# A five-layer convolution and attention kernel: the start of the attention stage, its first image, put in another order

## The chip, the cores and the metric

The kernel runs on one core of one Trainium2 chip, in one launch. The metric is the device time in microseconds (us), the median of several runs. Names of engines are those of the profile: PE is the TensorE matmul engine, PEld its weight loads, DVE is VectorE, ACT is ScalarE, POOL is GpSimd, SP is SyncE. Lines such as L1475 are lines of the kernel before.

## The reference, cut to what matters

Sixteen images of 256 channels and 28x28 pixels go through a binary 3x3 convolution, a second block of a 3x3 and a 1x1 binary convolution with gates, a third block of two binary 3x3 convolutions with batch norms, and attention over the pixels of each image. The end of the third block and the attention are where the change lies:

```python
    out = batchnorm(out, g3, b3)      # over all images: (x - m) * rsqrt(v + EPS) * g + b
    out = out + x                     # x: the input of this third block
    return prelu(out, a3)             # where(y >= 0, y, a3 * y)
...
    q = jnp.einsum('rc,bcn->bnr', Wq, xf)        # 64 rows out of 256 channels, 784 pixels
    k = jnp.einsum('rc,bcn->brn', Wk, xf)
    v = jnp.einsum('rc,bcn->bnr', Wv, xf)
    attn = jnp.einsum('bnr,brm->bnm', q, k) * scale
    attn = jax.nn.softmax(attn, axis=-1)
    out = jnp.einsum('bnm,bmr->brn', attn, v)
    out = jnp.einsum('cr,brn->bcn', Wp, out)
    return out.reshape(B, C, H, W) + x
```

The batch norm's statistics need the last convolution of the last image. So the first image's attention can start only once they are there.

## The kernel before, in words

`forward` runs the stages one after the other. An image is held as two channel halves of 128 partitions (`k` = 0, 1) by 784 pixels; the pixels in turn come in two halves of 392 (`cuts`, below "half one" and "half two", HN = 392). The products of the last convolution land in `pt`, the tiles that the profile calls `p`; the third block's input is `x2`, for the first two images loaded back into SBUF during the stage before (L488), for the others in DRAM as `x2d`.

After the last convolution `forward` issues `keep_busy(35)`, 35 matmuls of 128x512 on an idle tile whose result nobody reads (L502), and beside them `norm("l2c", ...)` (L234): DVE aggregates the statistics, ACT takes the square root (L143, in `rsqrt`), DVE makes the scale `sg3` (the profile's `l2c_r`) from it, and ACT makes the shift `bg3` (`l2c_shift`, L260).

`attend_unshifted` does the attention. Inside its `manual_schedule` each engine keeps the order in which the program issues its instructions, so the order of the Python calls is the order on each queue. The pieces that the change and the prediction name:

- Image 0 is made by hand (L1620 to L1630). Scale and x2 in one DVE step for channel half 1 (L1622, `x*sg3 + x2`, in both pixel halves first). Then, for each pixel half: `finish_a` on ACT for channel half 0 (L1453, `x*sg3 + bg3`), ACT's shift of channel half 1 (L1626), DVE's addition of x2 to channel half 0 (L1627), DVE's prelu of both channel halves (L1629, `max(alpha*y, y)`, which reads y twice), and `queries_keys` on PE (L1475): two fp32 matmuls of 128x128x392 give queries in PSUM partitions 0 to 63 and keys in 64 to 127 of one bank.
- An ACT instruction on two columns with `AF.Exp` (L1631) brings in the exp table ahead of its first use, and `keep_busy(8)` issues 8 more idle matmuls on PE (L1468).
- `keys_to` and `queries` copy keys and queries out of PSUM: keys twice, to partitions 64 to 127 by ACT and to 0 to 63 by DVE (both L1486), queries by ACT (L1482).
- `finish_a(1)` and `finish_b(1)` do the same for image 1 with all 784 pixels: ACT's `x*sg3 + bg3` (L1453), DVE's addition (L1461) and prelu (L1462). For images from 2 on, `finish_a` ends with a DMA on POOL's queue that adds x2d to the tile (L1455).
- `scores(b, c)` is chunk c of 7: two fp32 matmuls side by side (L1498) into a tile of the pool `ps_sc`, which has two buffers, and ACT's exp of 128x784 (L1502) into one of seven `es` buffers.
- `project_v` makes the values (L1561, 16 small matmuls, 32 in the profile, since it lists an fp32 matmul as two), ACT copies them (L1565), DVE transposes them (`turn_v`, L1571). `values(b, c)` multiplies them with an `es` chunk (L1519, tile `av`).
- `sum_up` adds `es` chunks: 0 to 3 on POOL (L1510, L1512), 4 to 6 on DVE.

Then comes the loop over b from 0 to 14. Pass b does the rest of image b's chunks, and makes image b+1's queries, keys and values, and images b+2 and b+3's `finish_b` and `finish_a`, in between.

```python
            scores(b, 1)
            ...
            scores(b, 3)
            sum_up(b, 2, 3)
            ps = two_banks(psmi, "mi")
            for h in range(2):
                queries_keys(b + 1, h, ps)
```

Of the kernel before, what the change touches and what calls it, by code (L numbers as in the profile page):

```python
# [27 lines left out]
F32 = mybir.dt.float32  # L28
# [5 lines left out]
AF = mybir.ActivationFunctionType  # L34
# [5 lines left out]
P = 128  # L40
# [46 lines left out]
def forward(ctx: ExitStack, tc: tile.TileContext, d: dict, out: bass.AP, careful: bool):  # L87
# [16 lines left out]
    def pv(name):  # L104
        return vec[:, VECS.index(name), :]
# [31 lines left out]
        V.tensor_tensor(o, a, b, op)  # L137
        return o

    def rsqrt(name, v, half=None, beside=None):  # L140

        r, t = (const.tile(list(v.shape), F32, name=name + q) for q in ("_r", "_t"))
        A.activation(t, v, AF.Sqrt)  # L143
        if beside:
            beside()
        V.reciprocal(r, t)
        tt(t, r, r, ALU.mult)
        if half is not None:
            tt(r, r, half, ALU.mult)
        else:  # L150
            V.tensor_scalar(r, r, -0.5, None, ALU.mult)
        tt(t, t, v, ALU.mult)
        V.scalar_tensor_tensor(r, t, -3.0, r, ALU.add, ALU.mult)
        return r
# [76 lines left out]
                V.bn_aggr(self.mv[:, k, :], self.fin[:, k, :])  # L231
            return self.mv[:, :, 0], self.mv[:, :, 1]

    def norm(name, moments, gamma, beta, sf=None, then=lambda r: None, late=False):  # L234


        half, e = vtile(name + "_half"), vtile(name + "_e")
        V.tensor_scalar(half, gamma, -0.5, None, ALU.mult)
        if sf is not None:

            tt(e, sf, sf, ALU.mult)
            V.tensor_scalar(e, e, 1e-30, 1.0 / EPS, ALU.max, ALU.mult)
            V.reciprocal(e, e)
        m, var = moments()
        v, c, less = vtile(name + "_v"), vtile(name + "_c"), vtile(name + "_less") if late else None
        if sf is not None:
            tt(v, var, e, ALU.add)
        else:
            V.tensor_scalar(v, var, EPS, None, ALU.add)
        r = rsqrt(name, v, half, (lambda: V.tensor_scalar(less, m, -1.0, None, ALU.mult)) if late else None)  # L250
        then(r)
        if not late:
            tt(c, m, r, ALU.mult)
            return r, tt(c, beta, c, ALU.subtract)

        def shift(b):
            o = vtile(f"{name}_shift{len(made)}")
            made.append(o)
            for k in range(2):
                A.activation(o[:, k:k + 1], r[:, k:k + 1], AF.Identity, bias=b[:, k:k + 1], scale=less[:, k:k + 1])  # L260
            return o

        made = []
        return r, shift
# [225 lines left out]
    with tc.tile_pool(name="ps_conv", bufs=3, space=PSUM) as psc, \  # L490
# [7 lines left out]
        def keep_busy(n):  # L498

            ps = pss.tile([P, 512], F32, tag="sm", name="unused")  # L500
            for _ in range(n):
                tc.keep_in_program_order(T.matmul(ps, lhsT=idle[:, 0:P], rhs=idle, start=True, stop=True))  # L502
# [706 lines left out]
        with tc.tile_pool(name="ph2", bufs=1) as ph:  # L1209
# [119 lines left out]
            if careful:  # L1329
                keep_busy(45)  # L1330
                sg3, bg3 = norm("l2c", mom, pv("g3"), pv("b3"), sf2)
                tt(bg3, bg3, cc, ALU.add)
            else:
                keep_busy(35)
                with tc.manual_schedule(engines={ET.DVE, ET.Activation}):
                    sg3, shift3 = norm("l2c", mom, pv("g3"), pv("b3"), sf2, late=True)
                    bg3 = shift3(b3c)


# [69 lines left out]
def attend_unshifted(ctx, tc, d, out, wqk, wv, wp, keys, worst, doubts, flag, pv, finish):  # L1409
# [40 lines left out]
    def finish_a(b, n=slice(0, N), ks=range(2)):  # L1450
        for k in ks:
            v = x[b][:, k, n]
            A.activation(v, v, AF.Identity, bias=bg3[:, k:k + 1], scale=sg3[:, k:k + 1])  # L1453
        if b >= 2 and 1 in ks:
            nc.gpsimd.dma_start(out=x[b], in_=x2d[b], accum_op=ALU.add)  # L1455
# [8 lines left out]
    def keep_busy(n):  # L1464

        ps = one_bank(pssm, "sm")
        for _ in range(n):
            T.matmul(ps, lhsT=idle[:, 0:P], rhs=idle, start=True, stop=True)  # L1468

    qs = [None] * B  # L1470

    def queries_keys(b, h, ps):

        for k in range(2):
            T.matmul(  # L1475
                ps[:, h, :HN], lhsT=wqk[:, k, :], rhs=x[b][:, k, h * HN:(h + 1) * HN], start=(k == 0), stop=(k == 1)
            )

    def queries(b, h, ps):
        if h == 0:  # L1480
            qs[b] = buf("q", 2, shape=(P, HN))
        A.copy(qs[b][64 * h:64 * h + 64], ps[0:64, h, :HN])  # L1482

    def keys_to(b, rows, h, ps):
        copy = A.copy if rows else V.tensor_copy
        copy(  # L1486
            keys[b % 2][64 * rows:64 * rows + 64, :, 2 * h:2 * h + 2, 0:GC].rearrange("p c g i -> p g c i"),
            ps[64:P, h, :HN].rearrange("p (g c i) -> p g c i", g=2, i=GC),
        )
# [80 lines left out]
    def turn_v(b):  # L1570
        V.transpose(va[b % 2].rearrange("p c r -> p (c r)"), vt.rearrange("p c a i -> p (c a i)"))  # L1571
# [44 lines left out]
    with tc.manual_schedule(engines={ET.PE, ET.Activation, ET.DVE, ET.Pool, ET.SP}):  # L1616

        ps = [two_banks(psmi, "mi"), two_banks(pssc, "sc")]
        cuts = [slice(h * HN, h * HN + HN) for h in range(2)]
        for n in cuts:  # L1620
            v = x[0][:, 1, n]
            V.scalar_tensor_tensor(v, v, sg3[:, 1:2], x2[0][:, 1, n], ALU.mult, ALU.add)  # L1622
        for h, n in enumerate(cuts):
            finish_a(0, n, (0,))
            v, w = (x[0][:, k, n] for k in range(2))
            A.activation(w, w, AF.Identity, bias=bg3[:, 1:2])  # L1626
            V.tensor_tensor(v, v, x2[0][:, 0, n], ALU.add)  # L1627
            for k, y in enumerate((v, w)):
                V.scalar_tensor_tensor(y, y, alpha[:, k:k + 1], y, ALU.mult, ALU.max)  # L1629
            queries_keys(0, h, ps[h])  # L1630
        A.activation(ph.tile([P, 2], F32, name="e"), sg3, AF.Exp, scale=0.0)  # L1631
        keep_busy(8)
        for h in range(2):
            keys_to(0, 1, h, ps[h])
            queries(0, h, ps[h])
            keys_to(0, 0, h, ps[h])
        finish_a(1)
        scores(0, 0)
        project_v(0)
        finish_b(1, ks=(0,))  # L1640
        turn_v(0)
        finish_b(1, ks=(1,))
        V.transpose(ones.rearrange("p a i -> p (a i)"), turned.rearrange("p a i -> p (a i)"))
        for b in range(B - 1):
            scores(b, 1)
            if b > 0:
                take_values(b - 1)
            if b == 0:
                finish_a(2)
            if b > 1:  # L1650
                project(b - 2, 0)()
            sum_up(b, 1)
            scores(b, 2)
            if b > 0:
                sum_up(b - 1, 6)
            scores(b, 3)
            sum_up(b, 2, 3)
            ps = two_banks(psmi, "mi")
            for h in range(2):
                queries_keys(b + 1, h, ps)  # L1660
            for h in range(2):
                keys_to(b + 1, 1, h, ps)
            for h in range(2):
                queries(b + 1, h, ps)
            for h in range(2):
                keys_to(b + 1, 0, h, ps)
            project_v(b + 1)
            if b > 0:
                sum_all(b - 1)
            turn_v(b + 1)  # L1670
            scores(b, 4)
            scores(b, 5)
            sum_up(b, 5)
            if b + 2 < B:
                finish_b(b + 2)
            if b + 3 < B:
                finish_a(b + 3)
            for c in range(4):
                values(b, c)
            if b > 0:  # L1680
                denominators(b - 1)
                invert(b - 1)
                normalize(b - 1)
            scores(b, 6)
            scores(b + 1, 0)
            if b > 1:
                project(b - 2, 1)()
                store(b - 2)
            if b > 0:
                watch(b - 1)  # L1690
            for c in range(4, NC_):
                values(b, c)


        b = B - 1
        scores(b, 1)
        take_values(b - 1)
        project(b - 2, 0)()
        sum_up(b, 1)
        scores(b, 2)  # L1700
        denominators(b - 1)
        invert(b - 1)
        scores(b, 3)
        sum_up(b, 2, 3)
        normalize(b - 1)
        scores(b, 4)
        scores(b, 5)
        sum_up(b, 5)
        scores(b, 6)
        project(b - 2, 1)()  # L1710
        store(b - 2)
        doubts_so_far()
        for mo in range(2):
            project(b - 1, mo, pool=pssc)()
        store(b - 1)
        watch(b - 1)
        for c in range(3):
            values(b, c)
        last = two_banks(pssc, "sc")
        denominators(b)  # L1720
# [214 lines left out]
```

## Time and profile before

| what | value |
|---|---|
| median of three runs | 949.11 us (948.44 to 949.25) |
| the profiled execution's own time | 949.33 us |
| its span in the profile | 947.5 us |
| PE busy | 930.7 us (98%) |
| DVE, ACT, POOL busy | 757.1, 675.1, 139.0 us |
| mean granted TensorE clock | 0.999 |
| idle matmuls ahead of attention, L502 | 35, from 661.07 us to 668.64 us |
| first attention matmul | 668.73 us |
| end of the queries and keys of image 0 | 671.79 us |
| queries and keys of image 1 begin | 678.65 us |

Times within the run are counted from the span's start. The span is 1.8 us shorter than the profiled execution's device time, and that execution is 0.2 us above the median. In the views that follow, a line of the chain of work gives start, length, and engine with tile and line; a line of the timeline gives start, length, engine, line, operation, out<-in, shapes, count and, in brackets, the idle time ahead of it with what ended it. Lengths in the timeline count a group of instructions from the first one's start to the last one's end.

### The profile page before, as it was taken

To read this page: it belongs to the slowest core of one execution; us is meant where nothing else is said; L and a number is where in the kernel's file an instruction comes from. 1 tells how busy PE (TensorE), PEld (TensorE's weight loads), DVE (VectorE), ACT (ScalarE), POOL (GpSimd) and SP (SyncE) were. 2 spreads that over 40 slices of the span, in tenths; PEclk is the share of its full clock that TensorE was granted. 3 is DMA by queue.
4 is the path that set the end of the run, shared out by engine and by line. 5 is a ranking of instruction groups with operands and counts; after the bars stand their busy time and mean duration, and the time that the engine had idled before them with its cause. 6 is when DMAs were issued, how large, how long until landed. Compare 5 with 4: busy or idle time off the path is not lost.

```text
span 947.5 us, 15043 instructions
## 1 busy us (share of the span) xinstructions
PE 930.7 (98%) x5636; PEld 583.2 (62%) x5636; DVE 757.1 (80%) x1446; ACT 675.1 (71%) x1179; POOL 139.0 (15%) x157
## 2 busy tenths in 40 slices
PE   7999999999999999999999999999999999999996
PEld 3555678788888878887555565556444444444442
DVE  3777798999998899987788878889656768687765
ACT  5665578888888888875777766775867666666652
POOL 2001100000000000000000000000334353534331
PEclk9999999999999999999999999999999999999999
DMA  9887434445533444421556211111132434434212
GB/s 346 287 303 264 168 121 138 165 181 198 198 139 139 148 156 164 160 86 50 223 209 214 113 40 59 79 78 59 35 68 70 112 92 94 112 78 126 69 68 106
DMA packets 39333, 130.70 MB, mean 138 GB/s; under 512 B 4866, under 2 KB 16324, under 8 KB 39252
## 3 DMA queue, kind: packets, MB, share of 16 engines
q1 hardware_dynamic: 33332, 98.31, 28.7%
q0 software_dynamic: 5632, 30.54, 11.7%
q8 instruction: 46, 0.75, 0.3%
q10 hardware_dynamic: 288, 0.80, 0.2%
q14 instruction: 35, 0.29, 0.1%
HBM read 72.67 MB, written 32.11 MB: 111 GB/s over the span
## 4 chain that ended last, share of the span: by engine, by line
PE 94%; DMA 1%; ACT 1%; DVE 1%; SPq 1%; issue 0%; DVEq 0%; ACTq 0%
PE cv L400 29%; PE cv L806 29%; PE sc L1498 8%; PE av L1519 8%; PE cv L933 5%; PE mi L1475 5%; PE sm L1561 2%; PE mi L1579 2%; PE unused L502 2%; PE sm L1519 1%; DMA xs<-in_x_dram 1%; PE gate L901 1%; PE hid L709 1%; DMA shifted<-fpads 1%; SPq L293 0%
## 5 line engine op out<-in xcount | busy, mean ns | idle before, releaser
L806 PE MATMUL cv<-vs,w 128*128 128x392 f32 (+1 forms) x1296 | 272.4, 352 | 0.3 <-DVE vs L137 0.3
L400 PE MATMUL cv<-fpads,wpk 128*128 128x392 f16 (+1 forms) x1458 | 247.8, 326 | 2.5 <-DVE wpk L325 1.2
L400 PEld LDWEIGHTS <-wpk 128*128 128x128 f16 x1782 | 171.5, 97 | 123.2 <-issue 3.1
L806 PEld LDWEIGHTS cv<-vs,w 128*128 128x128 f32 x768 | 143.2, 190 | 6.3
L1502 ACT ACTIVATE es<-sc 128x784 f32<-128x784 f32 x112 | 87.3, 822 | 41.4 <-PE sc L1498 41.4
L806 PEld LDWEIGHTS <-w 128*128 128x128 f16 x768 | 69.4, 99 | 51.9 <-issue 9.1
L1498 PE MATMUL sc<-q,keyswa 64*128 64x392 f32 x448 | 89.9, 513 | 0.9 <-ACT es L1502 0.9
L1519 PE MATMUL av<-es,v 128*64 128x392 f32 x448 | 80.7, 499 | 0.0
L1264 DVE SCALAR_TENSOR_TENSOR p<-ab,vec 128x392 f32<-128x392 int16 (+1 forms) x132 | 78.0, 605 | 0.0
L416 ACT ACTIVATE ab<-cv 128x392 int16<-128x392 f32 (+1 forms) x66 | 32.1, 486 | 56.3 <-PE cv L400 53.4
L1512 POOL TENSOR_TENSOR sum<-sum,es 128x784 f32<-128x784 f32 x32 | 67.2, 2099 | 3.1 <-ACT es L1502 0.6
L1498 PEld LDWEIGHTS sc<-q,keyswa 64*128 64x128 f32 x448 | 38.9, 186 | 44.0 <-issue 17.1
L400 PE MATMUL cv<-shifted,wpk 128*128 128x392 f16 (+1 forms) x324 | 60.6, 322 | 0.2 <-DMA shifted<-fpads 0.2
L806 PE MATMUL cv<-one_on,w 128*128 128x392 bf16 x240 | 59.4, 329 | 0.0
L961 POOL DMA_DIRECT2D x2d<-x x16 | 8.6, 536 | 345.3 <-DVE x L955 285.0
L1486 DVE COPY keyswa<-mi 64x392 f32<-64x392 f32 x31 | 16.3, 564 | 53.1 <-ACT q L1482 53.1
L1519 PEld LDWEIGHTS av<-es,v 128*64 128x64 f32 x448 | 29.4, 136 | 47.4 <-issue 47.0
L418 DVE SCALAR_TENSOR_TENSOR ab<-ab,cv 128x392 int16<-128x392 int16 (+1 forms) x66 | 36.0, 546 | 27.7 <-ACT ab L416 27.3
L788 ACT CAST vs<-vs 128x840 fp32r<-128x840 bf16 x63 | 54.1, 882 | 2.5 <-DVE vs L137 2.5
L933 PE MATMUL cv<-z,fw 128*128 128x392 f32 x256 | 48.9, 342 | 0.1
L933 PEld LDWEIGHTS cv<-z,fw 128*128 128x128 f32 x256 | 46.1, 188 | 0.9 <-ACT z L925 0.9
L1475 PE MATMUL mi<-p,wqk 128*128 128x392 f32 x124 | 45.1, 506 | 0.1
(323 smaller groups left out, 1531.2 us busy)
## 6 DMA issues: line engine op xcount, KB each, us to landing
xs<-in_x_dram SPq DMA_DIRECT2D x30, 784.0 KB, 5.1
one_on<-vs SPq DMA_DIRECT2D x60, 209.8 KB, 2.8
x2d<-x POOLq DMA_DIRECT2D x16, 784.0 KB, 3.6
out_dram<-p SPq DMA_DIRECT2D x15, 784.0 KB, 3.4
shifted<-fpads SPq DMA_DIRECT2D x26, 449.8 KB, 2.8
p<-x2d POOLq DMA_DIRECT2D x14, 784.0 KB, 6.7
p<-x2d SPq DMA_DIRECT2D x13, 784.0 KB, 5.7
n0d<-n POOLq DMA_DIRECT2D x16, 392.0 KB, 4.8
```

The source lines that it names most:

```text
L400: T.matmul(pss[j][:, n // size if careful else h, :rows * S].rearrange("p (a b) -> p a b", b=S), lhsT=w[:, n, c, :], rhs=src[:, blocks[j][ ...
L416: A.activation(by_halves(ab[:, 1], blocks[j]), ps, AF.Copy, scale=1.0 / PACK)
L418: V.scalar_tensor_tensor(a, b, -PACK, ps, ALU.mult, ALU.add)
L788: copy(v, w)
L806: T.matmul(ps.rearrange("p (a b) -> p a b", b=S), lhsT=w[:, k, c, u, mo * P:(mo + 1) * P], rhs=one_on[:, u, k, :, 0:S] if moved and c == 1 ...
L933: T.matmul(ps[:, h, :HN], lhsT=w[:, k, mo * P:(mo + 1) * P], rhs=z2[b][:, k, h * HN:(h + 1) * HN], start=(k + i == 0), stop=(k + i == 2),)
L1264: V.scalar_tensor_tensor(p, y, alpha[:, mo:mo + 1], y, ALU.mult, ALU.max, accum_out=mom.sums_at(at, mo)[0] if mom.by_sums(at, mo) else None,)
L1475: T.matmul(ps[:, h, :HN], lhsT=wqk[:, k, :], rhs=x[b][:, k, h * HN:(h + 1) * HN], start=(k == 0), stop=(k == 1))
L1498: T.matmul(ps[:, h, :HN], lhsT=chunk[rows], rhs=qs[b][rows], start=True, stop=True)
L1502: A.activation(e, ps[:, :, :HN], AF.Exp, scale=0.125)
L1512: (V if late else nc.gpsimd).tensor_tensor(sums[b, late], sums[b, late], e, ALU.add)
L1519: T.matmul(ps[64 * h:64 * h + 64, :HN], lhsT=w, rhs=e[:, h, :], start=start, stop=stop)
```

## The change

It is confined to the first image of attention and what leads to it. The norm's `rsqrt` gets an extra ACT instruction of two columns with `AF.Exp` right behind the square root, and the one at L1631 goes. The idle matmuls go from 35 to 31, and the 8 at L1468 go. Channel half 0 of pixel half one is made in the way of channel half 1 (one DVE step with scale and x2, then ACT's shift), as is channel half 1 of image 1. Pixel half two of image 0 gets its queries and keys by separate 64-column matmuls in two PSUM tiles (`queries_keys_apart`), of which the one for keys comes from `ps_sc`. The keys of half one are copied by ACT alone, those of half two by DVE alone. Image 0's values (`project_v`, `turn_v`) come ahead of its scores, chunks 0 to 3 of its scores and the first two of `values` come ahead of the loop, and `finish_a(2)` with its DMA on POOL's queue comes after `sum_up(0, 1)` and `sum_up(0, 2, 3)`.

```diff
-    def rsqrt(name, v, half=None, beside=None):
+    def rsqrt(name, v, half=None, beside=None, then=None):
         r, t = (const.tile(list(v.shape), F32, name=name + q) for q in ("_r", "_t"))
         A.activation(t, v, AF.Sqrt)
+        if then:
+            A.activation(small.tile(list(v.shape), F32, tag="mv", name="table"), v, then, scale=0.0)
...
-                keep_busy(35)
+                keep_busy(31)
                 with tc.manual_schedule(engines={ET.DVE, ET.Activation}):
-                    sg3, shift3 = norm("l2c", mom, pv("g3"), pv("b3"), sf2, late=True)
+                    sg3, shift3 = norm("l2c", mom, pv("g3"), pv("b3"), sf2, late=True, table=AF.Exp)
...
-    def queries_keys(b, h, ps):
+    def queries_keys(b, h, ps, ks=(0, 1)):
+        for k in ks:
+            T.matmul(
+                ps[:, h, :HN], lhsT=wqk[:, k, :], rhs=x[b][:, k, h * HN:(h + 1) * HN],
+                start=(k == ks[0]), stop=(k == ks[1]),
+            )
+
+    def queries_keys_apart(b, h, qps, kps):
         for k in range(2):
+            for i, ps in enumerate((qps, kps)):
+                rows = slice(64 * i, 64 * i + 64)
+                T.matmul(
+                    ps[rows, h, :HN], lhsT=wqk[:, k, rows], rhs=x[b][:, k, h * HN:(h + 1) * HN],
+                    start=(k == 0), stop=(k == 1),
+                )
...
-    def keys_to(b, rows, h, ps):
-        copy = A.copy if rows else V.tensor_copy
+    def keys_to(b, rows, h, ps, copy=None):
+        copy = copy or (A.copy if rows else V.tensor_copy)
...
-        for n in cuts:
-            v = x[0][:, 1, n]
-            V.scalar_tensor_tensor(v, v, sg3[:, 1:2], x2[0][:, 1, n], ALU.mult, ALU.add)
-        for h, n in enumerate(cuts):
-            finish_a(0, n, (0,))
-            v, w = (x[0][:, k, n] for k in range(2))
-            A.activation(w, w, AF.Identity, bias=bg3[:, 1:2])
-            V.tensor_tensor(v, v, x2[0][:, 0, n], ALU.add)
-            for k, y in enumerate((v, w)):
-                V.scalar_tensor_tensor(y, y, alpha[:, k:k + 1], y, ALU.mult, ALU.max)
-            queries_keys(0, h, ps[h])
-        A.activation(ph.tile([P, 2], F32, name="e"), sg3, AF.Exp, scale=0.0)
-        keep_busy(8)
-        for h in range(2):
-            keys_to(0, 1, h, ps[h])
-            queries(0, h, ps[h])
-            keys_to(0, 0, h, ps[h])
-        finish_a(1)
+        one, two = cuts
...
+        for k, n in ((1, one), (0, one), (1, two)):
+            to_x2(0, k, n)
+        for k in (1, 0):
+            shifted(0, k, one)
+            prelu(0, k, one)
+        queries_keys(0, 0, ps[0], (1, 0))
+        finish_a(0, two, (0,))
+        shifted(0, 1, two)
+        add_x2(0, 0, two)
+        for k in range(2):
+            prelu(0, k, two)
+        kps = two_banks(pssc, "sc")
+        queries_keys_apart(0, 1, ps[1], kps)
+        keys_to(0, 1, 0, ps[0])
+        queries(0, 0, ps[0])
+        keys_to(0, 0, 0, ps[0], A.copy)
+        queries(0, 1, ps[1])
+        for rows in range(2):
+            keys_to(0, rows, 1, kps, V.tensor_copy)
+        finish_a(1, ks=(0,))
+        to_x2(1, 1)
+        project_v(0)
+        turn_v(0)
         scores(0, 0)
-        project_v(0)
-        finish_b(1, ks=(0,))
-        turn_v(0)
-        finish_b(1, ks=(1,))
+        scores(0, 1)
+        shifted(1, 1)
+        add_x2(1, 0)
+        for k in range(2):
+            prelu(1, k)
+        sum_up(0, 1)
+        scores(0, 2)
+        scores(0, 3)
+        sum_up(0, 2, 3)
+        for c in range(2):
+            values(0, c)
+        finish_a(2)
         V.transpose(ones.rearrange("p a i -> p (a i)"), turned.rearrange("p a i -> p (a i)"))
         for b in range(B - 1):
-            scores(b, 1)
             if b > 0:
+                scores(b, 1)
                 take_values(b - 1)
...
-            for c in range(4):
+            for c in range(0 if b > 0 else 2, 4):
                 values(b, c)
```

`to_x2`, `shifted`, `prelu` and `add_x2` are the four steps that were written out before: DVE's scale and x2 in one, ACT's shift, DVE's prelu, DVE's addition. In the pass b = 0 the loop now begins at image 1's queries and keys; for b > 0 it is as before.

More of the change, by code (lines that the diff above doesn't have):

```diff
@@ L232, in __call__, with norm @@
             return self.mv[:, :, 0], self.mv[:, :, 1]
-    def norm(name, moments, gamma, beta, sf=None, then=lambda r: None, late=False):
+    def norm(name, moments, gamma, beta, sf=None, then=lambda r: None, late=False, table=None):
         half, e = vtile(name + "_half"), vtile(name + "_e")
@@ L249, in norm @@
             V.tensor_scalar(v, var, EPS, None, ALU.add)
-        r = rsqrt(name, v, half, (lambda: V.tensor_scalar(less, m, -1.0, None, ALU.mult)) if late else None)
+        r = rsqrt(name, v, half, (lambda: V.tensor_scalar(less, m, -1.0, None, ALU.mult)) if late else None, table)
         then(r)
@@ L1470, in attend_unshifted @@
     qs = [None] * B
-    def queries_keys(b, h, ps):
-        for k in range(2):
-            T.matmul(
-                ps[:, h, :HN], lhsT=wqk[:, k, :], rhs=x[b][:, k, h * HN:(h + 1) * HN], start=(k == 0), stop=(k == 1)
-            )
+    def queries_keys(b, h, ps, ks=(0, 1)):
[5 more added lines that the diff above has]
+    def queries_keys_apart(b, h, qps, kps):
+        for k in range(2):
+            for i, ps in enumerate((qps, kps)):
[4 more added lines that the diff above has]
+                )
     def queries(b, h, ps):
@@ L1631, in attend_unshifted, with to_x2 @@
-        A.activation(ph.tile([P, 2], F32, name="e"), sg3, AF.Exp, scale=0.0)
-        keep_busy(8)
-        for h in range(2):
-            keys_to(0, 1, h, ps[h])
-            queries(0, h, ps[h])
-            keys_to(0, 0, h, ps[h])
-        finish_a(1)
-        scores(0, 0)
-        project_v(0)
-        finish_b(1, ks=(0,))
-        turn_v(0)
-        finish_b(1, ks=(1,))
+        one, two = cuts
+        def to_x2(b, k, n=slice(0, N)):
+            v = x[b][:, k, n]
+            V.scalar_tensor_tensor(v, v, sg3[:, k:k + 1], x2[b][:, k, n], ALU.mult, ALU.add)
@@ new lines, in shifted, with prelu, add_x2 @@
+        def shifted(b, k, n=slice(0, N)):
+            v = x[b][:, k, n]
+            A.activation(v, v, AF.Identity, bias=bg3[:, k:k + 1])
+        def prelu(b, k, n=slice(0, N)):
+            v = x[b][:, k, n]
+            V.scalar_tensor_tensor(v, v, alpha[:, k:k + 1], v, ALU.mult, ALU.max)
+        def add_x2(b, k, n=slice(0, N)):
+            v = x[b][:, k, n]
+            V.tensor_tensor(v, v, x2[b][:, k, n], ALU.add)
+        for k, n in ((1, one), (0, one), (1, two)):
+            to_x2(0, k, n)
@@ L1646, in attend_unshifted @@
             if b > 0:
+                scores(b, 1)
                 take_values(b - 1)
[L1648 to L1654, printed above, removed]
+                if b > 1:
+                    project(b - 2, 0)()
+                sum_up(b, 1)
+                scores(b, 2)
                 sum_up(b - 1, 6)
-            scores(b, 3)
-            sum_up(b, 2, 3)
+                scores(b, 3)
@@ L1658, in attend_unshifted @@
+                sum_up(b, 2, 3)
             ps = two_banks(psmi, "mi")
```

## The prediction

> **What bounds the kernel now.** I read the page's chain first, then the chain in order of time between 660 and 720 us, then each engine's timeline there. The page's line by engine:
>
> ```profile
> PE 94%; DMA 1%; ACT 1%; DVE 1%; SPq 1%; issue 0%; DVEq 0%; ACTq 0%
> ```
>
> PE is the bound nearly everywhere, so a change pays only where PE's time is not real work. The chain by time shows where that is:
>
> ```profile
> 661.07 7.57 PE unused L502 x35
> 668.73 1.55 PE mi L1475 x4
> 670.28 1.51 PE sc L1475 x4
> 671.79 1.73 PE sm L1468 x8
> 673.54 0.93 PE sc L1498 x4
> 674.47 1.46 PE sm L1561 x32
> 675.94 0.88 PE sc L1498 x4
> 676.84 0.83 ACT es L1502
> 677.72 0.93 PE sc L1498 x4
> 678.65 2.83 PE mi L1475 x8
> ```
>
> PE does nothing of use until 668.64 (35 idle matmuls, `unused`) and from 671.79 to 673.52 (8 more, `sm` of L1468), and waits for an exp at 676.84 (0.83, the chain passes to ACT). From 678.65, where image 1's queries and keys begin, it is full. The timelines of DVE, then ACT, tell what it waits for:
>
> ```profile
> 665.95 1.16 DVE L1622 SCALAR_TENSOR_TENSOR p<-p,l2c_r,x 128x392 f32<-128x392 f32 x2
> 669.53 1.17 DVE L1629 SCALAR_TENSOR_TENSOR p<-p,vec 128x392 f32<-128x392 f32 x2
> 672.83 0.57 DVE L1486 COPY keyswa<-sc 64x392 f32<-64x392 f32 x1 [0.88 <-ACT q L1482]
> 668.87 1.28 ACT L1631 ACT_TABLE_LOAD   x1
> 672.82 1.97 ACT L1453 ACTIVATE p<-p,l2c_shift,l2c_r 128x784 f32<-128x784 f32 x2
> ```
>
> DVE has no gap over 0.1 from 665.95 to 670.70, when the last prelu of image 0 ends; PE's last queries-and-keys matmul ends 1.09 later, 671.79, with its weight load. The key copy on DVE waits until ACT has done its two. ACT's 1.97 us for image 1 stand ahead of exp 0, which starts at 674.70 though its scores ended at 674.47.
>
> One resource more, from a later pass (DVE, then POOL):
>
> ```profile
> 709.02 2.06 DVE L1512 TENSOR_TENSOR sum<-sum,es 128x784 f32<-128x784 f32 x1
> 708.38 1.87 POOL L1510 TENSOR_TENSOR sum<-es 128x784 f32<-128x784 f32 x1 [4.94 <-ACT es L1502]
> 710.32 4.39 POOL L1512 TENSOR_TENSOR sum<-sum,es 128x784 f32<-128x784 f32 x2
> ```
>
> DVE's addition takes 0.96 alone (at 689.20) and 2.06 here: POOL's ends at 710.25, DVE's 0.83 later. Then POOL's two take 4.39, not 2 x 1.85. So they take turns, and DVE, which was waiting, went ahead of POOL's next one.
>
> [...] The trace has 1.28 at 668.87 with the next instruction at 670.16[...]; I use 1.28. [...] The longest PE gap that I find in the new order is 0.7, so I price fewer idle matmuls at nothing; the trace, granted clock 1.00 throughout here, has no such gap to test it.
>
> **The change, part by part.**
>
> *Exp table behind the root.* The root ends at 665.06; load 1.28 and the two-column exp 0.22 put the shifts at 666.60 instead of 665.95, and ACT's first shift of x at 666.60 + 0.57 = 667.17, ended (0.60) at 667.77. DVE meanwhile does three L1622 steps at 0.58: 665.95 to 667.69. So the load is hidden but for 0.1. Without that cover it would cost 0.65. Taking it from 668.87 gives nothing either: ACT had it done at 670.38, queries were ready at 670.28.
>
> *Half one and two.* DVE: three scale steps, two prelus (0.59 each), one addition (0.57), two prelus: 667.80 + 1.18 + 0.57 + 1.18 = 670.72, against 670.70: one addition fewer, one scale step more. PE's half one ends at 668.97 + 1.09 = 670.05 (31 idle matmuls end 4 x 0.216 sooner, at 667.78: no limit). Half two in two tiles: four 64-column matmuls side by side, like L1519's (16 in 2.78, 0.70 for four), so it ends near 671.85, before 671.79. No gain up to here.
>
> *Copies and values.* ACT takes half one's keys and query from 670.15 to 671.6, then half two's query to about 672.2; DVE takes both keys of half two from another bank, without ACT: 671.9 to 672.95. PE fills this time with `project_v` (1.46, to about 673.3) where 8 idle matmuls stood. Scores 0 starts then, and exp 0 at about 674.2, since only one 1.04 of image 1 lies ahead on ACT.
>
> *Up to image 1.* PE's real work before, from 671.79 to 678.65: values 1.46 and four scores 0.93 + 3 x 0.76 = 3.21, in all 4.67 of 6.86. So 2.19 is slack. After: the same 4.67 and two `values` chunks, 1.39, that no longer come later; the waits for exps 0 and 1 are about 0.1. PE is at image 1's queries at 671.85 + 6.15 = 678.0, with 1.39 done in advance: gain 0.65 + 1.39 = 2.04. From there on queue order and PE load are as before, and PE stays full, so it would last to the end.
>
> *What is late next.* Image 1's second prelu (L1462, 1.03, reads its tile twice from SBUF). Count from T = 671.85, the end of image 0's keys on PE. DVE: two key copies (L1486, two in 1.05 at 683.39) to T+1.11, image 1's scale step (L1462's 1.03 for the like of it) to T+2.07. PE ends the values at T+1.46; ACT copies them 0.12 later (as at 676.06) in 0.48, to T+2.06. DVE: transpose from T+2.10 (L1571, 0.57 to the next start), addition from T+2.67 (L1461, 0.93, next 0.03 later), first prelu from T+3.63 to T+4.66. ACT: scores 0 end at T+1.46 + 0.88, exp 0 starts at T+2.36, exp 1, behind scores 1, at T+3.12 and ends at T+3.94; the shift of 784 (0.93, estimated from 0.60 at 392 and 0.82 for an exp of 784 with no pointer operand) ends at T+4.78. So DVE has a gap of about 0.15 before the second prelu. POOL's first sum is ready with exp 1 at T+3.97, moved ahead of `finish_a(2)`'s DMA, and waits behind the first prelu. It takes its turn at T+4.6 for 1.85; the second prelu ends at T+4.6+1.85+0.93 = T+7.38 = 679.2. PE's second matmul of image 1 ends 1.09 later, 680.3, not at 678.0 + 1.5 = 679.5: a stall of 0.8. The trace doesn't show L1462 beside a POOL sum; the bounds are 0 ([...]DVE's next goes first) and 2.9 (below). I take 0.8 since the one waiting won above.
>
> *POOL's queue.* The image 2 DMA moves behind three sums: before at 679.83, now near 679.1 + 2 x 1.85 = 682.8. It lands 6.7 later (median of L1455), 689.5, and two prelus make 691.6. PE wants the second at 693.59 - 1.25 + 0.7 = 693.0. Behind those prelus DVE has the sum of chunk 6 and image 2's key copies, which wait for PE anyway. Hidden by 1.4; without the prelu stall by 0.6. The same for `finish_a(2)` on ACT, moved behind exp 3: it ends near 680, before POOL is free.
>
> Sum: 2.04 - 0.8 = 1.25. Against the profiled execution: 949.33 - 1.25 = 948.08 (span 947.5 - 1.25 = 946.25); the median before is 0.22 lower, so I predict 947.9.
>
> **Rivals.**
> - *No turn is lost* on that prelu. For: DVE's next instruction starts 0.07 before its last one's end in the timeline. Against: the gap of 0.15. Gain 2.04: 947.1.
> - *POOL comes ahead of image 1's first prelu*, if DVE's chain is 0.34 later than I count (T+3.63 against T+3.97) or ACT's earlier. Then sum T+3.97 to 5.82, prelu to 6.75, the next sum, ready since exp 2 at T+5.5, to 8.55, second prelu 9.48 = 681.3; PE's matmul ends 682.4 instead of 679.5: stall 2.9, so 0.85 slower than before: 950.0. Against: DVE must lose 0.34 in a chain of 3.6 us of measured steps.
> [...]
>
> That the change does not do what it says is excluded: the order of the built kernel's instructions has one table load, behind the root, no wait of DVE's key copies on ACT, and POOL's sums ahead of the DMA.
>
> **How the numbers follow.** My forecast 0.47, no turn lost 0.30, POOL first 0.08, [...]a gain beyond 2.04 (the queries of image 0 ready sooner) 0.04, another loss 0.04. The range 946.7 to 949.5 takes in the first two with the spread of the runs before (0.8)[...]; it leaves out POOL first and other losses. About 0.2% (1.9 us) is what a measurement of this kernel can tell from no change. A gain of 1.25 lies within it, one of 2.04 just outside: faster 0.33 (two thirds of the second case, a fifth of the first for what my sums may be off, the larger gain), slower 0.06 (the other losses, a quarter of POOL first, for which 950.0 would have to be 1 short), same 0.61.
>
> **What would show it.** Right: the chain has the values, not idle matmuls, between image 0's keys and its scores; PE reaches image 1's queries near 678.0, waits there about 0.8 for a prelu, the first POOL sum takes 2.5 instead of 1.85, and the loop's second pass starts its scores 1.25 before 690.8. Wrong: a prelu of 784 at 1.03 throughout, a wait for L1455's DMA on DVE that reaches PE, a clock below 1.00 after 667.8, or ACT's shift after 667.9.

## The result and the profile after

| | before | changed |
|---|---|---|
| median of 22 runs each | 948.89 us (948.44 to 950.08) | 947.50 us (947.24 to 948.81) |
| ratio, 95% interval | | 0.9985 (0.998 to 0.9991) |
| profiled execution, its span | 949.33, 947.5 us | 947.97, 946.1 us |
| mean granted TensorE clock | 0.999 | 0.998 |

The change saves 1.4 us, 0.15%. In the profile the loop's second pass starts its scores on PE at 690.82 us before and at 689.62 after, 1.2 sooner, and PE keeps that lead to its end (L1607 starts at 939.47, its like after the change, L1620, at 938.26). The start of attention varies by up to 0.9 us from profile to profile, so below I count a *stage*: from DVE's first scale step of image 0 to that start on PE. It takes 690.82 - 665.95 = 24.87 us before and 689.62 - 666.13 = 23.49 after: 1.38 less. The stage began 0.18 later in the changed profile, and the span is 1.4 less; its last 0.2 lies behind PE's work.

The chain of the changed kernel in order of time, for the same stretch as before (line numbers are now those of the changed kernel; `sc L1487` is queries and keys of pixel half two, `sm L1574` the values, `p L1645` a prelu):

```profile
670.40 1.59 PE sc L1487 x8
...
673.21 1.03 DVE p L1637
674.25 0.56 DVE v L1584
674.80 0.87 DVE p L1649
675.70 1.03 DVE p L1645
676.74 2.57 DVE p L1645
679.35 2.24 PE mi L1477 x6
```

Before, this stretch was PE's but for one exp on ACT, with idle matmuls in it. Now PE has no idle matmuls between 670.40 and 679, and the chain runs over DVE: image 1 is made in one row of scale step, transpose, addition and two prelus, and at the end of the row PE waits for it. The second prelu takes 2.57 us where the first takes 1.03. PE's timeline shows how long PE waits:

```profile
676.78 1.54 PE L1532 MATMUL av<-es,v 128*64 128x392 f32 x8
678.25 0.93 PE L1477 MATMUL mi<-p,wqk 128*128 128x392 f32 x2
679.35 2.24 PE L1477 MATMUL mi<-p,wqk 128*128 128x392 f32 x6 [0.17 <-DVE p L1645]
689.62 1.59 PE L1511 MATMUL sc<-q,keyswa 64*128 64x392 f32 x8
```

The first two values chunks (L1532) are done ahead of image 1's queries and keys. Those begin at 678.25, and the 8 matmul passes end at 679.35 + 2.24 = 681.59. Before, they took 2.90 by the timeline, so without the wait they would end at 681.15: the wait costs 0.44. (The 0.17 in brackets is less, since the pause before 679.35 lies partly inside the modelled end of the matmul ahead.) The same places of PE's timeline before, for comparison:

```profile
678.58 2.90 PE L1475 MATMUL mi<-p,wqk 128*128 128x392 f32 x8
684.39 2.85 PE L1519 MATMUL av<-es,v 128*64 128x392 f32 x16
690.82 1.59 PE L1498 MATMUL sc<-q,keyswa 64*128 64x392 f32 x8
```

The other engines, POOL, DVE and ACT, at the places that matter:

```profile
675.95 2.52 POOL L1523 TENSOR_TENSOR sum<-es 128x784 f32<-128x784 f32 x1 [11.58 <-ACT es L1515]
678.55 4.40 POOL L1525 TENSOR_TENSOR sum<-sum,es 128x784 f32<-128x784 f32 x2
682.88 0.94 POOL L1457 DMA_DIRECT2D p<-x2d  x1
```

```profile
689.67 1.98 DVE L1464 SCALAR_TENSOR_TENSOR p<-p,vec 128x784 f32<-128x784 f32 x2 [3.16 <-DMA p<-x2d]
```

```profile
665.26 1.28 ACT L145 ACT_TABLE_LOAD   x1
666.55 0.20 ACT L145 ACTIVATE table<-l2c_v 128x2 f32<-128x2 f32 x1
```

POOL's first sum is ready at 675.95, inside the first prelu, and takes 2.52 where a sum took 1.87 in the later pass. I read this as a sum that starts to move only when that prelu ends at 676.73; it is done at 678.47, 1.74 later. The second prelu ends 0.84 after it, at 679.31. Image 2's DMA is issued at 682.88, and DVE waits 3.16 for it, but PE does not wait for that prelu anywhere. The table load takes 1.28 and ends at 666.54, and ACT goes on at 666.55.

### The profile page after: what moved, and what is told of

It reads as the page before. It is cut to its first block, busy times and chain, and to the rows that moved or that the text cites. A ratio compares the mean times of both kernels' runs of the same rounds, so it can differ in the third digit from the quotient of the medians.

```text
span 946.1 us, 15020 instructions
## 1 busy us (share of the span) xinstructions
PE 928.1 (98%) x5623; PEld 581.7 (61%) x5628; DVE 758.0 (80%) x1446; ACT 674.8 (71%) x1179; POOL 140.9 (15%) x157
## 4 chain that ended last, share of the span: by engine, by line
PE 92%; DVE 3%; ACT 2%; DMA 1%; SPq 1%; issue 0%; DVEq 0%; ACTq 0%
PE cv L808 29%; PE cv L402 29%; PE sc L1511 8%; PE av L1532 8%; PE cv L935 5%; PE mi L1477 4%; PE sm L1574 2%; PE mi L1592 2%; PE sm L1532 1%; PE unused L504 1%; DMA xs<-in_x_dram 1%; PE gate L903 1%; PE hid L711 1%; DVE p L1645 1%; DMA shifted<-fpads 1%
## 5 line engine op out<-in xcount | busy, mean ns | idle before, releaser
L1532 PE MATMUL av<-es,v 128*64 128x392 f32 x448 | 81.0, 500 | 0.0
L1532 PEld LDWEIGHTS av<-es,v 128*64 128x64 f32 x448 | 29.3, 136 | 47.5 <-issue 46.8
```

The costliest lines, as they stand in the source:

```text
L1532: T.matmul(ps[64 * h:64 * h + 64, :HN], lhsT=w, rhs=e[:, h, :], start=start, stop=stop)
```

## Experiments

My theory after the result: PE gains 0.51 by being at image 1's queries sooner (12.12 us from the stage's start, 12.63 before) and 1.31 by the two values chunks done in advance (in the loop 16 passes took 2.78 by the chain, and the 8 that are left there take 1.47), in all 1.82; a lost turn between DVE's second prelu and POOL's sum takes 0.44 back. Rivals: the prelu is late for another reason than POOL (ACT's shift, the longer row on DVE); the gain comes from the idle matmuls that went, or from separate PSUM tiles, not from the values. Ratios below are to runs of the kernel before that were taken beside each experiment, with a 95% interval. The stage, from one profile each, tells the parts apart better than medians some tenths apart. In the expectations e1 is the run with the sums behind the DMA, e5 the one with the exp table at its old place, and e6 the one that joins the two.

### The sums behind the DMA

```diff
-        sum_up(0, 1)
         scores(0, 2)
         scores(0, 3)
-        sum_up(0, 2, 3)
         for c in range(2):
             values(0, c)
         finish_a(2)
+        sum_up(0, 1, 2, 3)
```

> The changed kernel with POOL's three sums of image 0 put behind image 2's DMA on POOL's queue, as they stood before the change. My theory: the second prelu of image 1 no longer stands behind a POOL sum, takes 1.03 instead of 2.57, and PE's stall of 0.5 ahead of image 1's second matmul goes: 1.9 us less than before the change, 0.5 less than the changed kernel. DVE's addition of chunk 5 then waits for POOL, hidden. Rival (the stall belongs to ACT's shift or to PE, not to the turn): no change against the changed kernel, 1.4 less than before.

Measured: 947.17 us, ratio 0.9979 (0.9971 to 0.9987); stage 688.32 - 665.27 = 23.05, 1.82 less than before. DVE's two prelus and PE's queries and keys of image 1 in this run:

```profile
674.83 2.08 DVE L1645 SCALAR_TENSOR_TENSOR p<-p,vec 128x784 f32<-128x784 f32 x2
```

```profile
677.39 2.90 PE L1477 MATMUL mi<-p,wqk 128*128 128x392 f32 x8
```

Two prelus take 2.08 instead of 3.60, and PE's eight passes are one group of 2.90 with no wait, 12.12 us after the stage's start, as in the changed kernel. So the stall of 0.44 goes and nothing comes in its place. It is POOL's sum that makes the prelu late. Which of POOL's effects, this run doesn't tell; the next one does.

### The second prelu with one SBUF input

```diff
-        for k in range(2):
-            prelu(1, k)
+        prelu(1, 0)
+        v = halves(x[1][:, 1, :])
+        V.scalar_tensor_tensor(
+            v, v, alpha[:, 1:2], ps[0][:, 0, :HN].unsqueeze(1).to_broadcast([P, 2, HN]), ALU.mult, ALU.max
+        )
```

> The changed kernel, but image 1's second prelu takes its second tensor from PSUM (the queries and keys of image 0, half one, twice), so that it has one SBUF tensor input; the prelu of that channel half of image 1 is thereby left out and replaced by a maximum with other data. My theory (two SBUF tensor inputs of DVE and a POOL sum exclude each other): the prelu takes about 1.03 beside a POOL sum, and the time is 1.9 us less than before the change. Rival (POOL holds up any DVE instruction of this length): the prelu still takes 2.5, and 1.4 less than before.

Measured: 947.05 us, ratio 0.998 (0.9972 to 0.9988); stage 688.97 - 665.93 = 23.04, 1.83 less. DVE, then POOL, which keeps its order here:

```profile
675.49 1.04 DVE L1645 SCALAR_TENSOR_TENSOR p<-p,vec 128x784 f32<-128x784 f32 x1
676.55 1.03 DVE L1680 SCALAR_TENSOR_TENSOR p<-p,vec,mi 128x784 f32<-128x784 f32 x1
```

```profile
675.74 2.52 POOL L1523 TENSOR_TENSOR sum<-es 128x784 f32<-128x784 f32 x1 [11.57 <-ACT es L1515]
```

The sum is where it was and takes its 2.52, from 675.74 to 678.26. The second prelu lies wholly beside it and takes 1.03, where the one that reads its tile twice from SBUF took 2.57. So it is not POOL's work as such, nor ACT's shift, but the second SBUF input, here a second reading of the same tile.

### Without the eight idle matmuls

```diff
         A.activation(ph.tile([P, 2], F32, name="e"), sg3, AF.Exp, scale=0.0)
-        keep_busy(8)
         for h in range(2):
```

> The kernel before without its 8 idle matmuls at L1468, nothing else. My theory: scores 0 wait for DVE's last key copy (ends 673.40) anyway, PE only idles; no change, within 0.2 us. Rival (the idle matmuls themselves cost 1.7, and their removal is the gain): 1.7 us less. A third reading (an idle stretch of 1.7 lowers the granted clock): slower, with the clock below 1.00 after 673.

Measured: 949.04 us, ratio 1.0001 (0.9992 to 1.0009); stage 690.28 - 665.41 = 24.87, as before. PE waits for the key copy in their place:

```profile
673.01 0.93 PE L1498 MATMUL sc<-q,keyswa 64*128 64x392 f32 x4 [1.75 <-DVE keyswa L1486]
```

The idle matmuls were a filling; taking them out earns nothing, and what matters is what is put in. The third reading is refuted too: behind this pause of 1.75 us PE's matmuls take what they took in the kernel before, the first four of the scores 0.93 and the values 1.53, and the mean clock of the profiled run is 0.997, that of the kernel before beside it 0.997 or 0.998 in 47 of 52 runs.

### The kernel before, with the values first

```diff
-        keep_busy(8)
         for h in range(2):
...
-        scores(0, 0)
         project_v(0)
+        scores(0, 0)
         finish_b(1, ks=(0,))
```

> The kernel before with project_v(0) put ahead of scores(0, 0) in place of the 8 idle matmuls: one part of the change alone. My theory: PE does 1.46 of real work while the copies run, but image 1's chain on ACT and DVE then limits PE: about 1.0 us less than before. Rivals: 1.4 less (this move is the whole gain), or no change (image 1's prelus bind already).

Measured: 948.14 us, ratio 0.9992 (0.9985 to 0.9998); stage 689.98 - 665.87 = 24.11, 0.76 less. PE at the second chunk of scores:

```profile
675.86 1.64 PE L1498 MATMUL sc<-q,keyswa 64*128 64x392 f32 x8 [0.80 <-ACT es L1502]
```

Work of 1.46 fills the hole, but PE then waits 0.29 for keys, 0.80 for an exp and 0.31 inside image 1's queries and keys (3.21 instead of 2.90): ACT has the two `finish_a(1)` steps, 1.97, and the values' copy ahead of exp 0. The whole change, which leaves one 1.04 there and makes more of PE's work ready, gets 0.62 more. The two parts don't simply add up, as the next run shows.

### The first values chunks back in the loop

```diff
-        for c in range(2):
-            values(0, c)
         finish_a(2)
...
-            for c in range(0 if b > 0 else 2, 4):
+            for c in range(4):
```

> The changed kernel with the first two values chunks put back into the loop's first pass. My theory: PE then waits for image 1's second prelu with nothing to do, and does the 1.39 later: the gain goes, 0 against before (within 0.3). Rival (it does not matter where these 1.39 of work stand): 1.4 less than before.

Measured: 948.82 us, ratio 1.0 (0.9992 to 1.0008); stage 690.47 - 665.67 = 24.80, 0.07 less than before. PE in the place of the stall:

```profile
676.33 0.93 PE L1477 MATMUL mi<-p,wqk 128*128 128x392 f32 x2
678.89 2.24 PE L1477 MATMUL mi<-p,wqk 128*128 128x392 f32 x6 [1.64 <-DVE p L1645]
```

PE gets to image 1 at 676.33, 10.66 us after the stage's start instead of 12.63 before, and then waits for the prelu. The whole gain of the change goes with these two lines of code: what was won ahead of them pays only if PE has work until image 1 is made.

This holds as long as the second prelu loses its turn to POOL's sum, as it does in this run too (3.60 for the two prelus, 2.51 for the sum). With the sums behind the DMA the second prelu ended 676.91 - 665.27 = 11.64 after the stage's start. My estimate from these figures, with PE's six passes ended 2.28 after the prelu as in the changed kernel and the rest as in this run: 11.64 + 2.28 instead of 681.13 - 665.67 = 15.46, so a stage of about 23.26, 1.6 less than before without any values chunk done in advance. That run was not made. If it is right, the two chunks mostly cover a wait that the order of POOL's sums brings in.

### The exp table at its old place

```diff
-                    sg3, shift3 = norm("l2c", mom, pv("g3"), pv("b3"), sf2, late=True, table=AF.Exp)
+                    sg3, shift3 = norm("l2c", mom, pv("g3"), pv("b3"), sf2, late=True)
...
         shifted(0, 1, two)
+        A.activation(ph.tile([P, 2], F32, name="e"), sg3, AF.Exp, scale=0.0)
         add_x2(0, 0, two)
```

> The changed kernel with the exp table load not behind the root but on ACT behind half two's shift, ahead of the copies, near its old place. My theory: ACT's copies come 0.6 later, the values' copy and DVE's transposition 0.45 later, so image 1's first prelu would start near 676.1, while POOL's first sum is ready near 676.0: POOL comes first, both prelus lose a turn, and PE waits about 2 us more: 0.7 us more than before the change. If the prelu keeps ahead: 1.4 less, as the changed kernel. Rival (the place of the load is worth its 0.65 on the path by itself): 0.8 less than before.

Measured: 947.67 us, ratio 0.9998 (0.999 to 1.0005). The median hides a spread of runs: 11 lie at 947.09 to 947.67, 5 at 948.73 to 949.33, and 5 at 950.24 to 952.28. The profiled execution (949.14) is one of the middle five, with a stage of 690.81 - 665.72 = 25.09, 0.22 more than before. DVE, PE and POOL in it:

```profile
675.20 5.30 DVE L1645 SCALAR_TENSOR_TENSOR p<-p,vec 128x784 f32<-128x784 f32 x2
```

```profile
678.01 0.93 PE L1477 MATMUL mi<-p,wqk 128*128 128x392 f32 x2 [0.40 <-DVE p L1645]
680.55 2.24 PE L1477 MATMUL mi<-p,wqk 128*128 128x392 f32 x6 [1.61 <-DVE p L1645]
```

```profile
675.25 1.88 POOL L1523 TENSOR_TENSOR sum<-es 128x784 f32<-128x784 f32 x1 [11.28 <-ACT es L1515]
```

This is the rival "POOL comes ahead of image 1's first prelu": the sum takes its own 1.88, the prelus stand behind it and behind the next sum, 5.30 for both, and PE waits twice, 0.40 + 1.61 = 2.0 by the brackets. Against the same kernel with the sums out of the way (the next experiment, 22.75) the price is 25.09 - 22.75 = 2.34. The table load now stands ahead of ACT's copies of keys, queries and values, so DVE's transpose and with it the first prelu are 0.21 later against the end of image 0's keys on PE (675.20 - 671.23 = 3.97 us, 3.76 in the changed kernel), and the sum is as early as it was (4.02, 4.01). That the 11 shorter runs are the other outcome of the same race fits their times, but there is no profile of one. The five longest are longer than this outcome explains: four of them have a mean clock of 0.994 or 0.995, and single runs of the kernel before, which has no such race, reach 950.88. Their cause is open.

### The table at its old place and the sums behind the DMA

This run joins the edit of the last experiment and that of the first.

```diff
-... norm("l2c", mom, pv("g3"), pv("b3"), sf2, late=True, table=AF.Exp)
+... norm("l2c", mom, pv("g3"), pv("b3"), sf2, late=True)
+        A.activation(ph.tile([P, 2], F32, name="e"), sg3, AF.Exp, scale=0.0)
...
-        sum_up(0, 1)
-        sum_up(0, 2, 3)
+        sum_up(0, 1, 2, 3)
```

> As e5, with POOL's sums behind image 2's DMA as in e1. My theory: without the turns the place of the load is hidden: 1.9 us less than before, within 0.2 of e1. Rival (the load's place is worth 0.65 by itself): 1.2 less.

Measured: 946.89 us (946.04 to 947.97), ratio 0.9978 (0.9968 to 0.9988); stage 688.33 - 665.58 = 22.75, 2.12 less than before and 0.30 less than with the sums moved alone. PE's first matmul of attention, with the table at its old place, then with the table behind the root (the first experiment):

```profile
667.97 1.56 PE L1477 MATMUL mi<-p,wqk 128*128 128x392 f32 x4 [0.58 <-DVE p L1645]
```

```profile
667.91 1.55 PE L1477 MATMUL mi<-p,wqk 128*128 128x392 f32 x4 [0.83 <-DVE p L1645]
```

Counted from DVE's first scale step (665.58 and 665.27) these are 2.39 and 2.64. So the load behind the root costs: it holds up the shifts, and DVE's first prelu waits 0.16 for ACT. Once the sums are out of the way, the old place is the better one in the profiles. By the medians against their own runs of before (2.05 and 1.78 saved) the two don't differ beyond their intervals; the 0.30 rests on one profile of each.

### Joint queries and keys in half two

```diff
-        kps = two_banks(pssc, "sc")
-        queries_keys_apart(0, 1, ps[1], kps)
+        queries_keys(0, 1, ps[1])
...
-        for rows in range(2):
-            keys_to(0, rows, 1, kps, V.tensor_copy)
+        keys_to(0, 0, 1, ps[1])
```

with ACT's copy of half two's other keys in its place, and the sums as in the first experiment.

> As e1, with half two's queries and keys in one PSUM tile by 128-column matmuls, keys copied by ACT and then DVE behind ACT's copies, as before the change. My theory: scores 0 start 0.35 later and all up to image 1 with them: 1.5 us less than before (e1 less 0.35). Rival (the two tiles are worth nothing, project_v covers the copies): 1.9 less, as e1.

Measured: 947.21 us, ratio 0.9985 (0.9979 to 0.9992); stage 688.82 - 665.40 = 23.42, 0.37 more than in the first experiment. PE at the first scores:

```profile
673.01 1.59 PE L1511 MATMUL sc<-q,keyswa 64*128 64x392 f32 x8 [0.29 <-DVE keyswa L1499]
```

With one tile DVE's copy waits for ACT's, and PE for it, which is the serial order that the prediction read from the kernel before. The copy starts at 672.29, when ACT's copy of the queries has ended (672.26), not already at the end of ACT's copy of the keys (671.77). The medians alone would not separate this run from the first experiment, so the 0.37 too rests on one profile of each.

### Fewer idle matmuls ahead of attention

Two runs of the kernel with the table at its old place and the sums behind, with none and with 20 of the 31 idle matmuls.

```diff
-                keep_busy(31)
+                keep_busy(20)
```

> The fastest version so far (e6: table load at its old place, sums behind the DMA) without any idle matmuls ahead of attention, so that PE has an idle stretch of about 7.3 us. [...]the granted clock falls in that stretch[...]; image 0's queries and keys, values and first scores take longer: 0 to 0.5 us less than before the change instead of 2.1 less, clock below 1.00 between 668 and 672. Rival (the idle matmuls are not needed here): 2.1 less, clock 1.00.

> The same with 20 idle matmuls instead of 31, an idle stretch of 0.57 + 11 x 0.216 = 2.9 us[...]: no change against e6, 2.1 us less than before the change, clock 1.00. Rival (any stretch longer than the changed kernel's 0.83 costs clock): up to 1.5 us more than that.

Measured: none 948.37 us, ratio 0.9998 (0.9989 to 1.0006), stage 690.58 - 665.57 = 25.01; 20 of them 947.95 us, ratio 0.999 (0.9982 to 0.9999), stage 690.99 - 665.40 = 25.59. PE's first matmul of attention with 20, then two stretches of that run (length, then busy time and count of PE, PEld, DVE, ACT and POOL, granted clock, DMA share and GB/s), and then one of the run with 31:

```profile
667.78 2.95 PE L1477 MATMUL mi<-p,wqk 128*128 128x392 f32 x4 [2.95 <-DVE p L1645]
```

```profile
668.00:670.00 2.00, 2.00 (x4) 0.93 (x4) 1.82 (x4) 1.86 (x3) 0.00 (x0) 0.50 0.00 0
672.00:674.00 2.00, 2.00 (x14) 0.62 (x14) 0.38 (x1) 0.72 (x2) 0.00 (x0) 0.51 0.00 0
```

```profile
668.00:670.00 2.00, 1.97 (x8) 0.81 (x8) 1.97 (x4) 1.97 (x4) 0.00 (x0) 1.00 0.00 0
```

With none, PE stands still for 7.18 us, until 667.87, and the clock is 0.50 from 668 to 672, 0.78 on the mean from 672 to 674 and 1.00 from 674 to 676. The idle matmuls do pay: 25.01 - 22.75 = 2.26 us, and all 13 runs have a mean clock of 0.992 to 0.994. If the clock of the profiled run went from 0.50 to 1.00 in one step, the mean of 0.78 puts that step near 672.9, about 5 us after PE's first matmul; this is an estimate. The expectation had the clock below 1.00 only until 672. The profiled run with 20 loses more, since its clock comes back later: 0.51 from 672 to 674, where the run with none has 0.78. With 20 the gap is 2.95, and I expected no loss. That was wrong: in the profile the clock is at half until about 674. It is not so in each run: 3 of the 13 runs, at 946.65 to 946.93 with a mean clock of 0.997, lose nothing against the kernel with 31; the 7 at 947.82 to 948.25 had 0.995 or 0.996, and the 3 at 949.23 to 949.55 had 0.994. What decides it run by run is open.

## Why the prediction held, step by step

Predicted were 947.9 us and 1.25 less than the profiled execution; measured 947.50 and 1.36 less in it (949.33 - 947.97). The mechanism held: work in place of idle matmuls, PE sooner at image 1, a part given back to a turn of POOL. That the sum came within 0.13 of the stage's 1.38 is partly luck, as the terms show.

- *The gain on PE.* Predicted 0.65 + 1.39 = 2.04. Measured 0.51 + 1.31 = 1.82, by the run with one SBUF input too (1.83). Both terms were a little high: the second exp is waited for with 0.29 where I had put about 0.1 for both, and 8 of the 16 values passes take 1.47, so what no longer comes later is 1.31, not half of 2.78.
- *The stall.* Predicted 0.8, measured 0.44. The step was right: the second prelu takes 2.57 behind a turn of POOL, which takes 2.52 (predicted 0.93 behind 1.85, ended 679.2; measured 679.31 in a stage that began 0.18 later). The term that was most too big is PE's time after the prelu. I put 1.09 to the end of the second matmul and the rest behind it at full pace, 4 more passes of 2.83 / 8 = 0.35, so 2.5 to the end; the six passes end 681.59 - 679.31 = 2.28 after the prelu, 0.22 less. The rest is small: counted from the stage's start the prelu ends up to 0.1 sooner than predicted (13.18), and PE is at image 1 0.07 later (12.12). The errors of gain and stall, -0.22 and +0.36, partly cancel; the net is 1.38 instead of 1.25.
- *Why the turn is lost.* I argued from two things: the side that waits had won its turn at 710.25, and DVE would have a gap of 0.15, ACT's shift being late. The first held. The gap is not there: the shift ends at 676.71, the first prelu at 676.73, the second is recorded from 676.74. POOL took its turn all the same. So what I held against the rival "no turn is lost" was wrong, and that the gap was not needed was luck. The rival, whose case was that DVE's next instruction follows at once, is refuted for this place: in both profiles the side that was waiting went ahead of the next instruction of the side that had the turn.
- *"POOL comes ahead of image 1's first prelu"* is real. My margin for it was 0.34; it is 0.25 (3.76 and 4.01 from the end of image 0's keys), and a table load in another place eats it: in one profile, and by their times in some 5 to 10 of 21 runs. Its price is 2.34, not 2.9.
- *The exp table* was held to be hidden but for 0.1 and to give nothing at either place. DVE waits 0.17 for the shift, near the 0.1, but the effect was not followed on: PE's start is 0.25 later with the load behind the root, and the stage 0.30. In the changed kernel it has a use that I did not see: it helps to keep the first prelu ahead of POOL's sum, by 0.25 in the profiles instead of 0.05 with the load at its old place.
- *The table load* was taken at 1.28, as in the kernel before. It takes 1.28 here too, with 0.01 us to ACT's next instruction (666.54 to 666.55), as at the old place (670.15 to 670.16). The case that it costs more, 0.07 of the forecast, did not come.
- *Half one and two* gave nothing, as predicted: image 0's keys end 5.81 after the stage's start, 5.84 before. Two readings on the way were off, without effect. Four matmuls of 64 columns are 8 passes in the profile, 1.39 by the row that I used and not 0.70. And DVE before had one gap over 0.1: 0.14 at 667.11, behind the scale steps.
- *Copies.* In the kernel before, DVE's copy of half two's keys starts at 672.83, when ACT's copy of the queries has ended (672.80), about 0.5 us after the end of ACT's copy of the keys (672.31). The run with joint queries and keys has the same order (672.29, behind 672.26 and not 671.77). No run took that 0.5 us out, so what two tiles gain over one tile without that wait is open.
- *POOL's queue.* The DMA was predicted at about 682.8 and is at 682.88. It is hidden, as predicted: DVE waits 3.16 for it, PE not at all.
- *Fewer idle matmuls at nothing.* Right for this change: PE's longest gap there is 0.83, and with that the clock stayed at 1.00. That a gap of 0.7 costs nothing was my estimate, which no gap in the trace of the kernel before could test. It can't be carried to a longer gap: behind 2.95 the clock was 0.50 in the profiled run, while behind 1.75 (the kernel before without its eight idle matmuls) PE's matmuls took no longer than before.

## What to carry to other kernels

When work is moved into a hole of the bound engine, follow the next step that this engine needs, and what holds that step up. Here the next step, image 1's second prelu, was late by a lost turn, so the whole gain hung on other work for PE until it was made; a third as much again (0.44 of a stage) lay in three POOL sums that could go a few instructions later. Look for DVE instructions with two SBUF inputs next to POOL work on a path that counts; one lost turn made a prelu of 1.03 take 2.57 here, while with one SBUF input it took 1.03 beside the same sum, and, as the times of one experiment suggest, the order of turns can be a race that is won in some runs only. Filler matmuls should be cut by the gap that is left, and the clock read in the profile afterwards.

## What the runs showed of the hardware beyond what was expected

- With both sides waiting in turn, DVE and POOL alternated instruction by instruction (at 710.25 before and 676.73 after), even where DVE's next instruction was ready 0.01 to 0.02 us after its last. In the run with the table at its old place the first prelu is recorded from 675.20 and the sum from 675.25, and still the sum went first: it took its own 1.88, the prelu 2.6 to 2.8. So the recorded time of an instruction that needs its turn can include its wait, and the recorded starts don't tell who goes first at this distance.
- Behind a pause of PE of 2.95 us the clock was 0.50 or 0.51 for about 6 us of matmuls in the profile (668 to 674), and 10 of the 13 runs show a loss by time and mean clock. Behind the pause of 0.83 us of the changed kernel it was 1.00 (668 to 676), and behind one of 1.75 us four matmuls of scores took 0.93, as without it. What lies between 1.75 and 2.95 was not tried.
